# Two rooms for the column sums of a turn

## Chip, cores and metric

The kernel runs on one core of a Trainium2 chip. The metric is the device time of one execution in microseconds (us), the median of several runs.

## What is computed

The reference is a model of four layers on an input of 4 images of 96 channels and 64 x 64 pixels. The change lies in layer 0, a selective scan over the pixels in four directions:

```python
xf = u.reshape(b, DI, L)                              # rows, forwards
xt = u.transpose(0, 1, 3, 2).reshape(b, DI, L)        # columns, forwards
xs = jnp.stack([xf, xt, jnp.flip(xf, -1), jnp.flip(xt, -1)], axis=1)
...
hst = hst * dA + (dt_ * ut)[..., None] * bt[:, :, None, :]
y = jnp.einsum('bkdn,bkn->bkd', hst, ct)
...
y1 = ys[:, 1].reshape(b, DI, w, h).transpose(0, 1, 3, 2)
y3 = jnp.flip(ys[:, 3], -1).reshape(b, DI, w, h).transpose(0, 1, 3, 2)
y = y0 + y1 + y2 + y3
```

Directions 1 and 3 run along columns, so their results have to be transposed before they can be added to those of directions 0 and 2, which run along rows. The sum then goes through a norm and a projection (`scan_outputs`, `output_norm`). Layer 1 is a convolution block, layer 2 a spectral block with a feed-forward part, layer 3 a linear attention with another.

## The kernel before

**Scans.** There are 4 images, 4 directions each, 4 steps of 1024 pixels for each direction, and 24 units in a step (6 groups of 32 channels, with 4 of the 16 states on the 128 partitions each time, 4 such sets): 1536 units. A unit is one product on GpSimd (POOL, L1280), one exponential on ScalarE (ACT, L1287), one scan on VectorE (DVE, L1303) and one product with the output coefficients on DVE or POOL (L1318). TensorE (PE) sums the products over the states (L1341). ACT copies the sums to `yt`, and they are stored to `d_y` in device memory. The operands of the units (`scan_d`, `scan_g`, `scan_B`, `scan_C`) are loaded from device memory on SyncE's queue (SP, L1265), all of them at fixed units of a step.

**The planner.** Function `scans` walks the units one by one; a unit's turn in that walk is called a slot here. After a slot's own instructions it lets other work in. That work is a list of stages in order (`front`, `weights`, `turn`, `conv`, `spectral`, `layer_2`, `product`, `layer_3`, or `layer_3_turn` where a turn shares a stage with layer 3). Only the first stage on the list is served. A stage holds streams (Python generators), a few of them active at once. A stream yields the engine that its next piece needs with a planned time, or `wait(n)`, which holds that stream for n slots. `advance` takes a piece if its engine has room left in this slot. The planner hands out a planned rate of at least 6.0 us a slot; at the start of a step it raises the rate to the work left over the slots left, where that is more. The order of the instructions on every engine is thus fixed when the program is built, by counts and planned times alone. What is left of the stages after the last unit is issued without slots between.

**The turn.** `turn(b)` turns the column sums of image b into rows. There are four of them: for images 0 and 1 in stages of their own, for images 2 and 3 next to layer 3 of the image before. A turn has three thirds of 64 channels. Each one

- loads the sums of directions 1 and 3 for 64 channels and all 4096 pixels into the buffer `t` (L657; two loads of 1 MB, 64 partitions each). `t` is a tile of 128 x 6144 floats from `big`, a pool with two buffers that all stages share;
- waits for 10 slots;
- works on 8 chunks of 512 pixels: `fetch` loads the chunk's rows of direction 0 (L666) and of the skip connection (L667) into the tail of `t`, PE adds both directions while it reads `t` transposed (L672) and adds the rows (L674), ACT copies the result (L678), and it is stored to `d_yt`;
- waits for 2 slots, and the next third is loaded into the same `t`.

For the last image (`early`) the order of the thirds is 2, 0, 1. The chunks of its thirds 0 and 1 wait until direction 0 has come so far (`ready`).

After a turn comes the convolution block of the same image (`conv_block`). Its stream `scan_outputs` waits until enough of the image is scanned (`scanned[b] >= 4 * NCH - c`, which counts chunks over the four directions), then the sum, the norm and the projection follow. `expansions` (L806) and `rows` (L829, L845) are its matmuls; its memory is again two tiles from `big`.

Of the kernel before, what the change touches and what calls it, by code (L numbers as in the profile page):

```python
# [97 lines left out]
def hybrid_kernel(ctx: ExitStack, tc: tile.TileContext, a: dict):  # L98
# [3 lines left out]
    wait = lambda n: ("wait", n, 0, False)  # L102
# [17 lines left out]
    def turns(of):  # L120
        of.append(of.pop(0))
        return of[-1]
# [33 lines left out]
    def const(name, rows=slice(0, 128)):  # L156
        return cst[rows, CS[name]]
# [40 lines left out]
    def big(name):  # L198
        if last_room and turns(thirds) == "last":
            return last_room[0].tile([128, 6144], F32, name=name, tag="big", bufs=1)  # L200
        return bp.tile([128, 6144], F32, name=name, tag="big", bufs=2)
# [6 lines left out]
    def tmp(name, shape=(128, CH), dtype=F32):  # L208

        if last_room and dtype == F32:  # L210
            tag = turns(spare)
            if tag in LAST:
                return last_room[0].tile([128, CH], F32, name=name, tag=tag, bufs=LAST[tag])[:, : shape[1]]
        return bp.tile(list(shape), dtype, name=name, tag="tmp", bufs=TMP)
# [36 lines left out]
    def split(t):  # L251
        return t.rearrange("p (a b) -> p a b", a=RPC)
# [199 lines left out]
    def later(out, t, then=None):  # L452

        to_store.append((out, t, then))
# [8 lines left out]
    def ahead(n, first, items):  # L463

        items, got = list(items), []
        for i, item in enumerate(items):
            while len(got) < min(i + 1 + n, len(items)):
                got.append(first(items[len(got)]))
            yield item, got[i]

    def in_turn(items, make, matmuls, take, evict, depth=2, ready=None):


        made = []

        def oldest():
            p, item, at = made.pop(0)
            yield take[:3] + (at,)
            evict(p, item)
            free()  # L480

        items, n = iter(items), 0
        while True:
            while ready is not None and not ready(n):
                yield wait(1)
            item = next(items, None)
            if item is None:
                break
            yield make[:3] + (n > 0,)
            p = bank()  # L490
            matmuls(p, item)
            made.append((p, item, clock[0]))
            n += 1
            if len(made) == depth:
                yield from oldest()
        while made:
            yield from oldest()
# [148 lines left out]
    def turn(b):  # L646


        im = b % 2
        early = b == B - 1  # L650
        while scanned[b] < (2 if early else 3) * NCH:
            yield wait(1)
        t = big("ya")
        for r in (2, 0, 1) if early else (0, 1, 2):
            lo = 64 * r
            for at, k in ((0, 1), (64, 3)):
                load(t[at : at + 64, :L].rearrange("p (c l) -> p c l", c=NCH),  # L657
                     d_y[k][im][:, lo : lo + 64, :].rearrange("c p l -> p c l"))

            rows = not (early and r == 2)  # L660
            held = slice(0 if rows else 64, 128)

            def fetch(c):
                u = t[:, L + c % 4 * CH : L + c % 4 * CH + CH]
                if rows:
                    load(u[:64], d_y[0][im][c, lo : lo + 64])  # L666
                load(u[64:], d_skip[b][c, lo : lo + 64])  # L667
                return u

            def added(p, of):  # L670
                c, u = of
                mm(split(p[:64]), lhsT=const("two")[:, :64],  # L672
                   rhs=t[:, :L].rearrange("p (w h) -> p h w", h=H)[:, c * RPC : (c + 1) * RPC, :], start=True, stop=False)
                mm(p[:64], lhsT=skips[held, r], rhs=u[held], start=False, stop=True)  # L674

            def stored(p, of):
                s = tmp("yrow")[:64]
                nc.scalar.copy(s, p[:64])  # L678
                later(d_yt[im][of[0]][lo : lo + 64], s)

            chunks = ahead(1, fetch, range(NCH))

            ready = (lambda n: scanned[b] >= 2 * NCH + min(n + 2, NCH)) if early and rows else (lambda n: True)
            yield wait(10)
            yield from in_turn(chunks, pe(2.7, 1), added, ac(0.6), stored, ready=ready)
            yield wait(2)

    def scan_outputs(b, done):

# [401 lines left out]
    def layers_2_and_3(b):  # L1091
# [87 lines left out]
        else:  # L1179
# [3 lines left out]
            Stage("product", 1, product()),  # L1183
            Stage("layer_3", 4 if b == B - 1 else 3, *(layer_3(c) for c in range(NCH))) if b not in (1, 2) else
            Stage("layer_3_turn", 4, turn(b + 1), *(layer_3(c) for c in range(NCH))),
        ]

# [33 lines left out]
    def middle(b):  # L1221

        return ([] if b >= 2 else [Stage("turn", 1, turn(b))]) + conv_block(b)
# [439 lines left out]
```

## Time and profile before

| | |
|---|---|
| median of 3 runs | 6037.62 us (6030.58 to 6042.55) |
| profiled execution | 6029.4 us, its span 6027.6 us |
| mean granted TensorE clock | 0.857 |
| busy: DVE, POOL, PE, ACT | 88%, 86%, 76%, 64% of the span |
| DMA | 1078 MB, 179 GB/s over the span |
| last scan starts | 5545.7 us |
| last convolution ends, last spectral part begins | 5757.4 us |

The page of a profile gives busy times of the engines, the costliest groups of instructions and the transfers. A group's line has the line of the kernel, the engine, the operation, what it writes and reads, and a count; then the total busy time in us, the mean of one in ns, and the idle time of the engine ahead of it with what ended that. A view by stretches gives the same busy times between two moments of the span. DMA issues are listed with the KB of one and the median time from issue to landing.

### The profile page before, as it was taken

What the parts mean: (1) busy time and instruction counts of PE and PEld (TensorE: products, weight loads), DVE (VectorE), ACT (ScalarE), POOL (GpSimd) and SP (SyncE); (2) the same over time, 40 slices, a digit from 0 to 9 for tenths busy, and PEclk for the clock granted to TensorE, in tenths of its full rate; (3) what the DMA queues carried; (4) which work ended last, traced back from release to release, by engine and by line L of the source; (5) the groups of instructions that cost most, each with busy time, mean ns of one, the idle gap of its engine ahead of it and who ended that gap; (6) DMA issues with size and microseconds to landing.
All of it is one profiled execution on the core that took longest, in us unless ns stands there. A gap on an engine that the chain in (4) does not pass through costs nothing. (4 is left out here: it accounts for less than half of the span.)

```text
span 6027.6 us, 78329 instructions
## 1 busy us (share of the span) xinstructions
PE 4564.8 (76%) x27668; PEld 1682.2 (28%) x27668; DVE 5280.0 (88%) x3583; ACT 3856.1 (64%) x6056; POOL 5154.5 (86%) x2219
## 2 busy tenths in 40 slices
PE   6743867755898776686568888768888877779998
PEld 2100212211222642121012246211222642112284
DVE  4999898899999899989999999999999999897045
ACT  4853776764665677877556657777666677665335
POOL 4987898999999999989999999999999999897000
PEclk9855978877999888797689989878999888789999
DMA  5654575667754654466776446557754664674101
GB/s 182 229 177 152 195 227 183 219 211 232 216 161 148 200 194 154 159 196 205 229 238 186 164 159 217 166 175 224 220 173 155 199 199 144 184 239 146 48 16 38
DMA packets 425084, 1078.44 MB, mean 179 GB/s; under 512 B 79378, under 2 KB 81268, under 8 KB 423540
## 3 DMA queue, kind: packets, MB, share of 16 engines
q1 hardware_dynamic: 424692, 1073.44, 56.0%
q8 instruction: 219, 3.59, 0.3%
q14 instruction: 173, 1.42, 0.1%
HBM read 857.02 MB, written 220.66 MB: 179 GB/s over the span
## 5 line engine op out<-in xcount | busy, mean ns | idle before, releaser
L1280 POOL TENSOR_TENSOR scan_w<-scan_g,scan_B 128x1024 f32<-128x1024 f32 x1536 | 3606.5, 2376 | 242.0 <-PE ps_y L1341 112.3
L1287 ACT ACTIVATE ps_da<-scan_d,aneg 128x1024 f32<-128x1024 f32 x1536 | 1714.4, 1116 | 324.3 <-DVE scan_w L1318 176.1
L1318 POOL TENSOR_TENSOR scan_w<-scan_w,scan_C 128x1024 f32<-128x1024 f32 x676 | 1605.4, 2375 | 153.3 <-ACT state L1315 102.4
L1303 DVE TENSOR_TENSOR_SCAN ps_da<-ps_da,state,scan_w 128x1024 f32<-128x1024 f32 x633 | 1483.0, 2343 | 103.8 <-ACT ps_da L1287 92.5
L1341 PE MATMUL ps_y<-scan_w,cst 128*32 128x512 f32 x6144 | 1003.0, 730 | 590.8 <-POOL scan_w L1318 297.8
L1303 DVE TENSOR_TENSOR_SCAN scan_w<-ps_da,state,scan_w 128x1024 f32<-128x1024 f32 x519 | 1214.2, 2341 | 32.9 <-ACT ps_da L1287 30.7
L1318 DVE TENSOR_TENSOR scan_w<-ps_da,scan_C 128x1024 f32<-128x1024 f32 x860 | 1053.1, 1225 | 71.7 <-DMA scan_C<-bc 6.4
L1303 DVE TENSOR_TENSOR_SCAN ps_da<-ps_da,scan_w 128x1024 f32<-128x1024 f32 x227 | 518.4, 2284 | 58.3 <-ACT ps_da L1287 51.1
L1341 PEld LDWEIGHTS ps_y<-scan_w,cst 128*32 128x32 f32 x6144 | 147.2, 117 | 1221.5 <-POOL scan_w L1318 505.1
L1315 ACT COPY state<-ps_da 128x1 f32<-128x1 f32 x654 | 104.1, 159 | 488.4 <-DVE scan_w L1318 486.5
L829 PE MATMUL ps_mm<-h,wd 128*32 128x512 f32 x3144 | 363.5, 593 | 7.0 <-ACT r L169 7.0
L1303 DVE TENSOR_TENSOR_SCAN scan_w<-ps_da,scan_w 128x1024 f32<-128x1024 f32 x157 | 357.8, 2279 | 9.5 <-ACT ps_da L1287 6.9
L567 PE MATMUL ps_mm<-xp,taps 128*128 128x512 f32 x576 | 285.9, 639 | 51.6 <-ACT xp L547 22.2
L806 PE MATMUL ps_mm<-wd,w 128*32 128x512 f32 x1944 | 243.1, 613 | 17.9 <-ACT h L810 8.7
L618 PE MATMUL ps_mm<-xd,dtw 128*128 128x512 f32 x256 | 165.4, 737 | 70.8 <-ACT z L640 43.8
L1315 ACT COPY state<-scan_w 128x1 f32<-128x1 f32 x498 | 93.2, 187 | 192.0 <-DVE scan_w L1303 191.6
L627 ACT ACTIVATE z<-ps_mm 128x512 f32<-128x512 f32 x192 | 114.4, 596 | 148.3 <-PE ps_mm L622 76.5
L633 DVE SCALAR_TENSOR_TENSOR ps_mm<-ps_mm,z 128x512 f32<-128x512 f32 x192 | 131.3, 684 | 87.7 <-ACT z L631 82.6
L888 PE MATMUL ps_mm<-r,cst 128*128 128x512 f32 x220 | 149.4, 768 | 62.4 <-ACT r L885 13.8
L672 PE MATMUL ps_mm<-ya,cst 128*64 128x512 f32 x192 | 183.2, 1043 | 9.1 <-ACT acc L912 8.6
L810 ACT ACTIVATE h<-ps_mm 128x512 f32<-128x512 f32 x258 | 150.6, 596 | 53.8 <-PE ps_mm L806 50.9
L829 PEld LDWEIGHTS ps_mm<-h,wd 128*32 128x32 f32 x3144 | 110.6, 109 | 239.8 <-issue 207.3
(360 smaller groups left out, 6536.9 us busy)
## 6 DMA issues: line engine op xcount, KB each, us to landing
scan_g<-du SPq DMA_DIRECT2D x384, 512.0 KB, 5.0
scan_d<-delta SPq DMA_DIRECT2D x384, 512.0 KB, 5.9
scan_B<-bc SPq DMA_DIRECT2D x256, 512.0 KB, 5.3
scan_C<-bc SPq DMA_DIRECT2D x256, 512.0 KB, 5.2
y<-yt SPq DMA_DIRECT2D x384, 128.0 KB, 2.7
du<-g SPq DMA_DIRECT2D x128, 256.0 KB, 3.0
delta<-z SPq DMA_DIRECT2D x128, 256.0 KB, 2.8
tab<-in_etab SPq DMA_DIRECT2D x112, 256.0 KB, 4.0
```

What stands on the lines that cost most here:

```text
L567: mm(p, lhsT=taps[:, t, 0:128], rhs=window(t, c + e), start=t == 0, stop=t == 8)
L618: mm(p, lhsT=dtw[:, o + 2 * third, 0:128], rhs=xd, start=True, stop=True)
L672: mm(split(p[:64]), lhsT=const("two")[:, :64], rhs=t[:, :L].rearrange("p (w h) -> p h w", h=H)[:, c * RPC : (c + 1) * RPC, :], start=True, ...
L806: mm(p[32 * n : 32 * n + 32], lhsT=w1[:, 32 * g : 32 * g + 32], rhs=xin[:, n : n + 15 : 2, 1 : W + 1], start=True, stop=True)
L810: act(h[:, :, 1 : W + 1], split(p), AF.Relu)
L829: mm(p[32 * n : 32 * n + 32], lhsT=held["wd"][:, groups[i], o, dx, :], rhs=here[i][:, :, dx : dx + W], start=dx == 0, stop=dx == 2)
L1280: nc.gpsimd.tensor_mul(x["w"], x["step"]["g"][x["i"]], x["step"]["B"][x["j"]])
L1287: act(x["da"], x["step"]["d"][x["i"]], AF.Exp, scale=aneg[:, av : av + 1])
L1303: nc.vector.tensor_tensor_scan(x["h"][:, order], x["da"][:, order], x["w"][:, order], start, ALU.mult, ALU.add)
L1315: nc.scalar.copy(step["last"][:, u : u + 1], x["h"][:, end : end + 1])
L1318: x["made"] = engine.tensor_mul(x["w"], x["h"], x["step"]["C"][x["j"]])
L1341: done = mm(y[32 * q : 32 * q + 32], lhsT=const("stack"), rhs=group[m]["w"][:, e * CH : e * CH + CH], start=first, stop=last)
```

## The change

A turn takes two tiles from `big`. The loads of a third (`columns`) go to them in turn. The first third's loads are issued at the start, as before, and 8 slots later, ahead of its chunks, those of the second third. From then on the loads of the next third are issued when a third begins, and 2 slots later its chunks begin. The one wait of 10 slots in each third becomes 8 + 2 in the first third and 2 in the others; the wait of 2 slots behind each third becomes one behind the last.

```diff
         while scanned[b] < (2 if early else 3) * NCH:
             yield wait(1)
-        t = big("ya")
-        for r in (2, 0, 1) if early else (0, 1, 2):
-            lo = 64 * r
+        order = (2, 0, 1) if early else (0, 1, 2)
+        places = [big("ya"), big("yb")]
+
+        def columns(n):
+            t, lo = places[n % 2], 64 * order[n]
             for at, k in ((0, 1), (64, 3)):
                 load(t[at : at + 64, :L].rearrange("p (c l) -> p c l", c=NCH),
                      d_y[k][im][:, lo : lo + 64, :].rearrange("c p l -> p c l"))
 
+        columns(0)
+        for n, r in enumerate(order):
+            t, lo = places[n % 2], 64 * r
             rows = not (early and r == 2)
             held = slice(0 if rows else 64, 128)
 ...
             chunks = ahead(1, fetch, range(NCH))
 
             ready = (lambda n: scanned[b] >= 2 * NCH + min(n + 2, NCH)) if early and rows else (lambda n: True)
-            yield wait(10)
+            if n == 0:
+                yield wait(8)
+            if n + 1 < len(order):
+                columns(n + 1)
+            yield wait(2)
             yield from in_turn(chunks, pe(2.7, 1), added, ac(0.6), stored, ready=ready)
-            yield wait(2)
+        yield wait(2)
```

## Prediction

> **What bounds the kernel now.** I read the page's busy shares first, then its costliest groups, then busy time by stretch for the stages that the change touches, then the transfers beside the column loads, and last the chain that ended last.
>
> ```profile
> PE 4564.8 (76%) x27668; PEld 1682.2 (28%) x27668; DVE 5280.0 (88%) x3583; ACT 3856.1 (64%) x6056; POOL 5154.5 (86%) x2219
> ...
> L1280 POOL TENSOR_TENSOR scan_w<-scan_g,scan_B 128x1024 f32<-128x1024 f32 x1536 | 3606.5, 2376 | 242.0 <-PE ps_y L1341 112.3
> ...
> L1303 DVE TENSOR_TENSOR_SCAN ps_da<-ps_da,state,scan_w 128x1024 f32<-128x1024 f32 x633 | 1483.0, 2343 | 103.8 <-ACT ps_da L1287 92.5
> ```
>
> Each of the 1536 scan units occupies one slot of the program. It costs DVE a scan (2.34 us) and POOL a product (2.38 us), and a second product runs on either: 1.23 us on DVE (L1318, 860 times) or 2.37 us on POOL (676 times). So both engines stay full until the last scan at 5545.7 us. Everything else is filler that the planner slips between slots. After the last scan only TensorE is busy, with what filler is left.
>
> I walked the planner's loop slot by slot, and took the n-th L1303 on DVE as slot n's time. That gives the stretches below. Columns: us of the stretch, then busy time and count of PE, PEld, DVE, ACT, POOL, granted clock, DMA share, GB/s. First turn, third turn with layer 3, fourth turn with layer 3:
>
> ```profile
> 1311.00:1498.60 187.60, 110.55 (x336) 18.75 (x336) 183.33 (x102) 91.77 (x151) 183.53 (x80) 0.73 0.77 229
> 4023.80:4237.00 213.20, 167.97 (x486) 37.81 (x482) 195.50 (x118) 158.54 (x253) 201.17 (x88) 0.87 0.72 215
> 5142.80:5366.50 223.70, 179.46 (x488) 39.30 (x480) 194.08 (x116) 158.22 (x252) 197.53 (x86) 0.81 0.68 201
> ```
>
> The reader is to see that in the turn alone (first line, 60 slots, 3.13 us a slot) DVE and POOL are busy for 98% although the turn itself is mostly waiting: the scans go on. In the third line DVE is busy for 87%: there filler holds up the scans. The end of the program, from the first expansion of the last image's convolution to the last scan, and from there to the end of that convolution:
>
> ```profile
> 5454.00:5545.70 91.70, 87.97 (x548) 26.32 (x540) 87.06 (x53) 56.34 (x77) 83.87 (x36) 1.00 0.43 127
> 5545.70:5757.40 211.70, 200.42 (x1250) 58.48 (x1252) 16.72 (x29) 74.30 (x118) 2.35 (x1) 0.97 0.20 60
> ```
>
> PE is at 96% and 95%: from 5454 us on TensorE sets the time. The transfers around the second column load of the first turn (1360 to 1390 us; KB each, us from issue to landing), and the time of that load alone (1378 to 1384 us):
>
> ```profile
> ya<-y SPq DMA_DIRECT2D x2, 1024.0 KB, 14.3
> scan_C<-bc SPq DMA_DIRECT2D x3, 512.0 KB, 16.7
> ...
> 1378.00:1384.00 6.00, 2.61 (x16) 0.49 (x16) 5.80 (x5) 2.75 (x5) 6.00 (x4) 0.50 1.06 204
> ```
>
> A column load of 2 MB fills all DMA engines at about 200 GB/s, and a scan operand issued near it lands after 16.7 us, not the 5.2 us that the page has as scan_C's median.
>
> **What the Trainium skill says.** "Perfetto Trace Analysis", Identifying the Most-Contended Engine, judges Vector and GpSimd by occupancy, and its Optimization Strategy says that the contended engine may change between regimes. The trace agrees: DVE and POOL at 98% in the turn, PE at 95% at the end. "DMA: Bandwidth & Descriptors", Queues, rings and completion order, says that one issuer's descriptors are consumed in ring order on each DMA engine. The 16.7 us of scan_C behind the column load fits. The same page's Bandwidth table has 1 MB into 128 partitions at 341 GB/s; this load, in two halves of 64 partitions, ran at 204, and that decides.
>
> **The change, part by part.**
>
> *The waits.* Before, each third costs wait(10) and wait(2), 36 slots a turn; after, 8+2, 2, 2 and 2: 16. In the two turns that are stages of their own nothing else may run in those slots, so each stage shrinks from 60 slots to 40. No scan unit vanishes with a slot: 20 slots of 3.13 us are not 63 us saved, only filler moved forward by 20 slots. So what counts is where the earlier filler ends up. The walk gives (slots, before and after):
>
> ```
>                             before       after
> turn of image 0             293-352      293-332
> turn of image 1             757-816      745-784
> turn of image 3 + layer 3   1420-1480    1388-1459
> first expansion, last conv  1508         1504
> planned us left after slots 257          225
> ```
>
> Of the head start of 32 slots at the fourth turn only 4 are left at the first expansion. The last convolution reads scans of its own image: its first outputs wait until 26 chunks are scanned, the next until 28 (slot 1492 in both). After the change 22 of its slots stand empty.
>
> *The end.* It is costed in two ways. The walk takes 88 matmuls out of the part behind the last scan: 48 of L829 (4 pieces of the chain of 2.6 us, 10.4), 40 of L806 (10 pieces of 0.9 to 1.0, 9.5) and two of a norm (about 1): 21 us. But they go under the last 38 slots, where PE is already at 96%, and would stretch those. The second way counts from the first expansion, where TensorE begins to bind: it comes 4 slots earlier, and slots 1504 to 1508 took 13.0 us; the sums of 4 more slots (L1341, 0.65 us of PE a slot) fall behind it, 2.6 us. That is 10.4 us, and up to 3 more, since PE idled 3.7 us in that stretch. I take **-12**, bounds -8 and -21.
>
> *The fourth turn beside layer 3.* Before, the planner is late there and raises its rate to 9.74 us a slot, then 6.26 and 7.07; after, it is 6.0, then 5.09, over 72 slots instead of 61. The cost of haste is read from the stretches as span less the mean of DVE's and POOL's busy time, less the 2.2% that even the idle turn loses: third turn 213.2 - 198.3 - 4.7 = 10.2 us, fourth 223.7 - 195.8 - 4.9 = 23.0. At the lower rate I expect the 10 of the third turn: **-12**, bounds -20 and 0 (if the loss comes from the column loads, it stays).
>
> *Column loads on top of work.* The loads are the same 24 of 1 MB. Eight of the twelve pairs now go out two slots (6.3 us) ahead of a third's first rows (L666, L667), and run beside its stores. On SP's queue they stand ahead of the operands of later slots. The third load waits on SP for the last matmul that reads its room, issued a slot or two before; I put that under 2 us, hidden by operands loaded 4 slots or more ahead. The shortest lead is that of scan_C, four slots and a scan: 4 x 3.13 + 2.34 = 14.9 us, against 16.7 us seen beside a column load, which cost nothing visible. The turn alone gets denser: its DMA share was 0.77 of 187.6 = 144 us of work; 20 slots' operands less (20/24 of 10.5 MB, at the 415 GB/s that they reach, 21 us; stores of y 3) leave 120 in 40 slots of 3.13, 125 us: 96%. In the second turn, at 0.84, it is 133 in 125, at the limit. ACT's copies of rows (L678) wait for PE, PE for the rows, and the next decay (L1287) stands behind those copies. Nothing of before shows this overlap; from the 2 us by which 16.7 already exceeds 14.9 I take about 1 us for each of eight loads, **+8**; bounds 0 and +40 (5 us each, the late rows' 10 us stall half hidden).
>
> *Nothing:* the second room. The two buffers of that size are free when a turn starts (front or spectral part done), and the convolution's load into one waits only for matmuls two slots old. The products split 677 to 676, as before.
>
> **Sum:** -12 - 12 + 8 = -16. The profiled execution took 6029.4 us (span 6027.6 and 1.8 around it), 8.2 below the median of 6037.62: 6029.4 - 16 = 6013.4 there, and 6037.6 - 16 = **6022** as a median.
>
> **Rivals.**
>
> 1. *The transfers stay hidden* (chance 0.25): the overlap costs nothing, and more than 12 at the end is won: -25 to -33, about 6009. For it: PE already stands 7 us at a third's first rows in the first turn, and DVE loses nothing. Against: DMA at 96% and more.
> 2. *Likeliest, as summed* (0.38): -16, between -8 and -24, 6022.
> 3. *The gain is spent* (0.22): no loss goes from the fourth turn, or the overlap costs 15 to 25; -4 to +8, about 6039. For it: the fourth turn's idle time begins right behind column loads, which stay.
> 4. *DMA becomes the bound of the turn* (0.15), slower. One mechanism, in the turns of images 0 and 1: at 96 and 106% the backlog of a column load never drains before the next, scan_C lands after 25 us, and each of eight loads costs 25 - 14.9 = 10 us, less the gap left by the wait, say 5: +40 - 24 = +16, 6054. It decides from 24/8 = 3 us a load, and is measurable from 4.5.
>
> That the change doesn't do what it says is excluded for the waits (the walk shows 40 slots).
>
> **How the numbers follow.** About 0.2% (12 us) is what a measurement of this kernel can tell. Faster than 6025.5: all of rival 1, and some 0.32 of the likeliest case with its 0.38 (it straddles): 0.57. Slower than 6049.7: most of rival 4 and a little of 3: 0.15. The rest, 0.28, within. The range from 6000 to 6050 leaves out the far part of rival 4 and the best of rival 1.
>
> **What would show it.** Right: the two turns take 40 slots and 125 to 133 us each with DVE at 95% or more; the fourth turn with layer 3 has DVE at 92% or more; last scan near 5541 us, last convolution done near 5741 us instead of 5757, and 270 us from there to the end as before. Wrong: DVE below 90% in the two turns with waits for scan_C or ACT (rival 4), or the last scan no earlier (rival 3). If the last scan comes 12 us earlier but the end more than 25, PE was not the limit under the last slots.

## The result and the profile after

The changed kernel takes **6090.05 us** (median; 6086.05 to 6098.0), the kernel before 6036.06 us beside it: a ratio of 1.0088, with an interval of [1.0072, 1.0104]. It is slower by about 54 us, where the forecast was 6022 us and a range up to 6050. Beside the kernel before on another chip it was 6087.66 to 6034.23 us, a ratio of 1.0094 [1.0077, 1.0111].

The page after, busy shares and the two groups of a scan unit (the line numbers are 9 higher than before; the last columns are busy time, mean ns of one, and the engine's idle time ahead of the group with what ended most of it):

```profile
PE 4576.1 (75%) x27668; PEld 1700.4 (28%) x27668; DVE 5279.9 (87%) x3582; ACT 3853.7 (63%) x6056; POOL 5154.8 (85%) x2220
...
L1289 POOL TENSOR_TENSOR scan_w<-scan_g,scan_B 128x1024 f32<-128x1024 f32 x1536 | 3601.6, 2369 | 326.8 <-PE ps_y L1350 179.9
...
L1312 DVE TENSOR_TENSOR_SCAN ps_da<-ps_da,state,scan_w 128x1024 f32<-128x1024 f32 x631 | 1478.7, 2343 | 147.2 <-ACT ps_da L1296 134.7
```

The work is the same, but for one product that moved from DVE to POOL, and as long as before (scan 2343 ns, product 2369 against 2376). What grew is the idle time ahead of it: POOL's before L1289 from 242.0 to 326.8 us, DVE's before this form of the scan from 103.8 to 147.2. DVE is kept waiting by ACT's decay, POOL by PE's sum.

The same six stretches, taken as in the prediction (columns as there: us of the stretch, then busy time and count of PE, PEld, DVE, ACT, POOL, granted clock, DMA share, GB/s). In order: turn of image 0, turn of image 1, third turn with layer 3, fourth turn with layer 3, first expansion to last scan, last scan to the end of the last convolution:

```profile
1314.40:1460.40 146.00, 92.32 (x248) 16.38 (x248) 122.80 (x68) 64.73 (x109) 121.83 (x54) 0.78 0.81 232
2894.50:3033.70 139.20, 92.62 (x248) 16.59 (x248) 123.00 (x69) 61.46 (x85) 120.93 (x53) 0.77 0.83 232
3957.00:4192.20 235.20, 168.55 (x480) 38.71 (x480) 196.88 (x118) 162.17 (x276) 199.97 (x87) 0.84 0.67 194
5114.20:5388.10 273.90, 185.99 (x524) 39.50 (x520) 227.25 (x134) 172.55 (x273) 231.46 (x101) 0.78 0.64 188
5528.20:5634.80 106.60, 102.42 (x647) 33.67 (x649) 100.37 (x63) 69.49 (x99) 97.29 (x42) 0.99 0.46 145
5634.80:5826.90 192.10, 179.91 (x1182) 57.99 (x1174) 14.60 (x24) 66.52 (x105) 2.36 (x1) 1.00 0.20 61
```

The two lone turns have their 40 slots, but take 146 and 139 us for 122 us of work of DVE and POOL. Before, 60 slots took 187.6 us for 183. DVE is busy for 84% and 88% of them, where 95% was expected, and for 83% of the fourth turn, where 92% was expected. The DMA share did not go to 0.96 and over: it is 0.81 and 0.83.

From here on the **loss** of a stage is its length less the mean of DVE's and POOL's busy time, taken record by record with each instruction counted from its recorded start to its end. This is the measure of the prediction without its 2.2%; for the stages above the two agree within 1.6 us.

| us | before | after | after, other chip |
|---|---|---|---|
| loss, turn of image 0 | -0.4 | 21.2 | 16.9 |
| loss, turn of image 1 | -0.2 | 14.9 | 15.2 |
| loss, third turn with layer 3 | 10.5 | 32.6 | 34.7 |
| loss, fourth turn with layer 3 | 24.0 | 40.1 | 39.5 |
| loss, all other stages | 170 | 190 | 180 |
| last scan starts | 5545.7 | 5634.8 | 5623.6 |
| last scan to the end of the span | 481.9 | 461.4 | 462.8 |

On the other chip, whose profiled execution lies near the median, the account is: turns +72, other stages +10, less filler under the scans -5, the end -19; together +59 us between the two spans. So **72 of the 83 us that were newly lost lie in the four turns**, and the expected gain at the end did arrive. Each column is one execution: two of the same kernel differ by 2.5 us in the turns and by 10 in the other stages.

**One loss followed through.** At 1378 us the second third of image 0's turn begins. The DMA issues on SP's queue after, around that moment (start us, us, engine, line, operation):

```profile
1378.99 0.65 SPq L659 DMA_DIRECT2D ya<-y  x1
1379.76 0.67 SPq L1274 DMA_DIRECT2D scan_C<-bc  x1
1380.47 0.61 SPq L1274 DMA_DIRECT2D scan_d<-delta  x1
1381.48 0.50 SPq L459 DMA_DIRECT2D yt<-yrow  x1
1382.18 0.47 SPq L671 DMA_DIRECT2D yb<-y  x1
1385.57 0.45 SPq L672 DMA_DIRECT2D yb<-skip  x1
1386.06 0.60 SPq L671 DMA_DIRECT2D yb<-y  x1
1390.34 0.44 SPq L672 DMA_DIRECT2D yb<-skip  x1
```

The columns of the third third (L659, the second of two loads of 1 MB) and two operands of the scans are issued just ahead of the first rows (L671, L672) of the chunk that PE takes up next:

```profile
1380.09 1.91 PE L677 MATMUL ps_mm<-yb,cst 128*64 128x512 f32 x2
1400.66 1.94 PE L679 MATMUL ps_mm<-yb,skips 128*64 128x512 f32 x2 [18.66 <-DMA yb<-skip]
```

The waits of after between 1386 and 1406 us (who waited for whom: us in total, times, longest):

```profile
PEld ps_mm L679 <- DMA yb<-y: 20.3, 1, 20.3
PE ps_mm L679 <- DMA yb<-skip: 18.7, 1, 18.7
ACT yrow L683 <- PE ps_mm L679: 17.1, 1, 17.1
POOL scan_w L1289 <- PE ps_y L1350: 14.0, 1, 14.0
DVE scan_w L1312 <- ACT ps_da L1296: 13.1, 1, 13.1
```

And ACT's own order after (start, us, engine, line; in brackets the idle time before it and what ended it):

```profile
1384.40 1.11 ACT L1296 ACTIVATE ps_da<-scan_d,aneg 128x1024 f32<-128x1024 f32 x1
1402.63 0.58 ACT L683 COPY yrow<-ps_mm 64x512 f32<-64x512 f32 x1 [17.12 <-PE ps_mm L679]
...
1403.30 1.12 ACT L1296 ACTIVATE ps_da<-scan_d,aneg 128x1024 f32<-128x1024 f32 x1
```

This is the chain to read. The rows of direction 0 land 18.0 us after their issue, those of the skip connection just behind them. PE has started the chunk (L677) and stands before L679, which adds the rows. ACT stands before its copy of that chunk (L683) for 17.1 us. Behind the copy, in ACT's fixed order, is the next decay (L1296), which DVE's scan needs: DVE idles 13.1 us. Behind L679 on PE are the sums (L1350) that free POOL's buffers: POOL idles 14.0 us. The kernel before had a shorter hold of this kind at the first third's rows, in its waits between 1332 and 1348 us:

```profile
PEld ps_mm L674 <- DMA ya<-skip: 9.0, 1, 9.0
```

There DVE did not stop for it, and POOL for 1.6 us. A hold of 9 us was all but covered by what stood ready; one of 18 to 20 us was not. After, one long hold follows in each of the four turns, at slots 315, 767, 1082 and 1410: gaps of 13.1, 6.9, 11.7 and 12.5 us on DVE, and of 14.0, 10.4, 11.8 and 16.6 on POOL. The mean of the two engines makes 48 us, where the turns lost 75 more than before; shorter gaps in the first thirds, at slots 307, 1072, 1393 and 1401, make some 22. On the other chip the holds stand at the same four slots.

"DMA: Bandwidth & Descriptors" of the Trainium skill, Queues, rings and completion order, has each DMA engine take the descriptors of one issuer in ring order. The trace fits. The six transfers issued from 1378.34 to 1382.18 us land in the order of their issue, at 1390.3, 1395.5, 1397.2, 1399.8, 1400.0 and 1400.2 us: ahead of the 128 KB of rows stand 2 MB of columns and 1 MB of operands, at some 200 GB/s. The prediction priced its loads by scan_C and brought late rows in only as its upper bound, at 10 us of which half was to be hidden.

A second limit shows in the same trace. Of the 2510 issues on SP's queue whose eighth predecessor has a recorded landing, none starts before that landing, though 202 of 2510 start before the seventh has landed. So at most eight transfers are under way, and a block that lands late holds back later issues as well: the skip rows of the next chunk go out at 1390.34, when the first column load of 1378.34 has landed after 12.0 us. In this hold it cost little, since the first rows were issued only 0.2 us late by it; the order on the queue decides.

### The profile page after: what moved, and what is told of

Same layout as the page of the kernel before. It is cut to its first block, busy times and chain, and to the rows that moved or that the text cites. A ratio compares the mean times of both kernels' runs of the same rounds, so it can differ in the third digit from the quotient of the medians.

```text
span 6096.2 us, 78316 instructions
## 1 busy us (share of the span) xinstructions
PE 4576.1 (75%) x27668; PEld 1700.4 (28%) x27668; DVE 5279.9 (87%) x3582; ACT 3853.7 (63%) x6056; POOL 5154.8 (85%) x2220
## 5 line engine op out<-in xcount | busy, mean ns | idle before, releaser
L1289 POOL TENSOR_TENSOR scan_w<-scan_g,scan_B 128x1024 f32<-128x1024 f32 x1536 | 3601.6, 2369 | 326.8 <-PE ps_y L1350 179.9
L1296 ACT ACTIVATE ps_da<-scan_d,aneg 128x1024 f32<-128x1024 f32 x1536 | 1715.1, 1117 | 342.9 <-DVE scan_w L1327 188.7
L1327 POOL TENSOR_TENSOR scan_w<-scan_w,scan_C 128x1024 f32<-128x1024 f32 x677 | 1603.8, 2369 | 157.4 <-ACT state L1324 105.5
L1312 DVE TENSOR_TENSOR_SCAN ps_da<-ps_da,state,scan_w 128x1024 f32<-128x1024 f32 x631 | 1478.7, 2343 | 147.2 <-ACT ps_da L1296 134.7
L1350 PE MATMUL ps_y<-scan_w,cst 128*32 128x512 f32 x6144 | 1003.2, 731 | 553.1 <-POOL scan_w L1327 305.7
L1350 PEld LDWEIGHTS ps_y<-scan_w,cst 128*32 128x32 f32 x6144 | 147.3, 117 | 1186.2 <-POOL scan_w L1327 505.9
L1324 ACT COPY state<-ps_da 128x1 f32<-128x1 f32 x653 | 103.8, 159 | 475.0 <-DVE scan_w L1327 473.3
L1312 DVE TENSOR_TENSOR_SCAN scan_w<-ps_da,scan_w 128x1024 f32<-128x1024 f32 x156 | 355.3, 2278 | 18.6 <-ACT ps_da L1296 14.9
L567 PEld LDWEIGHTS ps_mm<-xp,taps 128*128 128x128 f32 x576 | 115.0, 206 | 225.9 <-issue 156.0
```

Of the source, the lines that this page charges most:

```text
L567: mm(p, lhsT=taps[:, t, 0:128], rhs=window(t, c + e), start=t == 0, stop=t == 8)
L1289: nc.gpsimd.tensor_mul(x["w"], x["step"]["g"][x["i"]], x["step"]["B"][x["j"]])
L1296: act(x["da"], x["step"]["d"][x["i"]], AF.Exp, scale=aneg[:, av : av + 1])
L1312: nc.vector.tensor_tensor_scan(x["h"][:, order], x["da"][:, order], x["w"][:, order], start, ALU.mult, ALU.add)
L1324: nc.scalar.copy(step["last"][:, u : u + 1], x["h"][:, end : end + 1])
L1327: x["made"] = engine.tensor_mul(x["w"], x["h"], x["step"]["C"][x["j"]])
```

## Experiments

The theory: rows and other small loads that are needed at once stand behind a block of column loads, PE waits for them, and ACT's and PE's fixed order passes the wait on to the scans. It was set against rivals: the second room itself, the DMA engines' total load, and the place that filler has in the steps of the scans.

**The change again, on another chip.**

> The change itself again, beside the kernel before on this chip: 50 to 60 us slower than before, with the one long hold (15 to 20 us of PE at the second third's first rows) in each turn at the same slots as in its first profile.

Measured: 1.0094 [1.0077, 1.0111], with the losses of the table above. The loss belongs to the program, not to one chip or one execution.

**The next third's columns in pieces behind the rows.** Eight pieces, each behind a chunk's rows, instead of 2 MB ahead of them; the slots stay those of after.

```diff
+        def piece(n, c):
+            t, lo = places[n % 2], 64 * order[n]
+            for at, k in ((0, 1), (64, 3)):
+                load(t[at : at + 64, chunk(c)], d_y[k][im][c, lo : lo + 64])
...
                 load(u[64:], d_skip[b][c, lo : lo + 64])
+                if n + 1 < len(order):
+                    piece(n + 1, c)
                 return u
...
-            if n + 1 < len(order):
-                columns(n + 1)
             yield wait(2)
```

> The change, but the next third's columns come in eight pieces of 2 x 128 KB, one behind each chunk's rows, instead of 2 MB at once ahead of the first rows. The planner's slots are the same as in the change. Theory A (the first rows queue behind the 2 MB; PE, then ACT's copy, then the decays stand, 13 us in one third of each turn and 2 to 6 in others): the stalls go; turn stages back to some 127 us each, 15 to 30 us faster than the kernel before. Theory B (the loss comes from the filler's new place against the operand loads and from a turn that is too dense for the DMA engines): no better than the change, 40 us or more slower than before.

Measured: 6052.45 against 6030.96 us, 1.0035 [1.0023, 1.0048]. The losses of the turns are 8.2, 12.7, 27.8 and 30.8 us: 79.5 in all, against 108.8 after and 33.9 before. The hold of 20 us at the second third becomes 10.6, and the gaps behind it fall from 13.1 to 5.2 us on DVE and from 14.0 to 7.7 on POOL. It missed: theory A had it 15 to 30 us faster than before, and theory B no better than the change; it lies between. The block ahead of the rows carried more than half of the 54 us. What stays: a piece still stands ahead of the next chunk's rows, which are fetched only one chunk ahead.

**The rows earlier.** The rows of a third's first four chunks are fetched ahead of the block, and the others three chunks ahead instead of one. The block stays whole. The thirds of the last image that wait for their scan (`early and rows`) are left as they are: that turn is the control.

```diff
-            chunks = ahead(1, fetch, range(NCH))
+            soon = not (early and rows)
+            chunks, head = ahead(3 if soon else 1, fetch, range(NCH)), []
...
+            if soon:
+                head = [next(chunks)]
             if n + 1 < len(order):
                 columns(n + 1)
             yield wait(2)
-            yield from in_turn(chunks, pe(2.7, 1), added, ac(0.6), stored, ready=ready)
+            yield from in_turn(chain(head, chunks), pe(2.7, 1), added, ac(0.6), stored, ready=ready)
```

> The change, but in each third four chunks of rows are loaded ahead of the 2 MB of the next third (and rows then run three chunks ahead); the last image's thirds 0 and 1 stay as in the change, since their rows are not there yet. Same slots as in the change. Theory A: the 13 us stalls go in the turns of images 0, 1 and 2 and one stays in that of image 3: between 5 and 20 us faster than before. Theory B: no better than the change.

Measured: 6053.54 us, 1.0045 [1.0032, 1.0057]: better than the change, but the 5 to 20 us under the kernel before were missed. The losses of the turns are 5.3, 2.5, 22.6 and 39.2. Its stretches, turn of image 0, of image 1, and the control:

```profile
1311.40:1442.30 130.90, 91.70 (x248) 16.18 (x248) 122.31 (x68) 65.02 (x109) 123.31 (x54) 0.83 0.88 261
2874.20:3002.40 128.20, 90.81 (x248) 16.37 (x248) 122.47 (x69) 61.81 (x85) 123.07 (x54) 0.83 0.89 261
5066.70:5339.80 273.10, 183.79 (x524) 39.42 (x520) 227.26 (x134) 172.78 (x273) 231.69 (x101) 0.80 0.63 189
```

Both lone turns now take what the prediction gave them (125 to 133 us), with the same bytes in fewer us: the DMA share rises to 0.88 and 0.89 while the loss falls. The control is unchanged at 273 us. Its waits between 5150 and 5176 us show the chain of before the edit:

```profile
PEld ps_mm L679 <- DMA yb<-y: 19.2, 1, 19.2
ACT yrow L683 <- PE ps_mm L679: 18.3, 2, 17.5
...
DVE scan_w L1315 <- ACT ps_da L1299: 14.4, 1, 14.4
```

Where the rows go out ahead of the block, between 1366 and 1392 us, the same three engines:

```profile
PEld ps_mm L679 <- DMA yb<-y: 9.4, 1, 9.4
...
ACT yrow L683 <- PE ps_mm L679: 7.3, 4, 2.5
...
DVE ps_da L1315 <- ACT ps_da L1299: 0.8, 1, 0.8
```

PE still waits 9.4 us, but ACT never more than 2.5, POOL 2.5 and DVE 0.8. This is the theory shown by itself: the same loads, the same slots, the same waits in the program; only when the rows go out, against the large loads, differs.

**The two rooms with the long waits.** All 10 slots of wait in each third as before; the second third's columns are then issued at the turn's start, right behind the first's.

```diff
-            if n == 0:
-                yield wait(8)
             if n + 1 < len(order):
                 columns(n + 1)
-            yield wait(2)
+            yield wait(10)
             yield from in_turn(chunks, pe(2.7, 1), added, ac(0.6), stored, ready=ready)
-        yield wait(2)
+            yield wait(2)
```

> Two rooms, the next third loaded when a third begins, but the waits of before (10 and 2 slots in each third), so the slots are those of before. Theory A: the wait of 10 slots covers the load and the rows come after it, so the time is that of before within 10 us, though no load is waited for any more. Theory B: within 10 us as well. A third view, that a second room by itself costs something (a buffer taken from other stages, the load's wait on SP): 15 us or more slower.

Measured: 6055.32 us, 1.0041 [1.0027, 1.0055]; losses of the turns -0.4, 9.0, 22.7 and 28.8. Theories A and B both missed by some 14 us and more; the time fits the third view, that a second room costs something by itself, which the run with pieces below excludes. The waits between 5175 and 5200 us, in the fourth turn, show one of its long holds:

```profile
PEld ps_mm L964 <- DMA xc<-x: 16.4, 1, 16.4
ACT xc L966 <- PE ps_mm L964: 15.7, 1, 15.7
...
DVE ps_da L1310 <- ACT ps_da L1294: 12.9, 1, 12.9
```

It is the same chain with another victim. Two blocks, 4 MB, go out at once, and a small load of layer 3 (`xc`), which shares the stage, stands behind them. The rows need not be the ones that are late.

**One room with the short waits.** The load of a third goes back to its start and to one buffer; the waits are those of after.

```diff
-        places = [big("ya"), big("yb")]
+        places = [big("ya")]
...
-        columns(0)
         for n, r in enumerate(order):
-            t, lo = places[n % 2], 64 * r
+            columns(n)
+            t, lo = places[0], 64 * r
...
-            if n + 1 < len(order):
-                columns(n + 1)
             yield wait(2)
```

> One room as before, but the waits of the change (10 slots in the first third, 2 in the others): the same slots as in the change, with the load in front of its own third. Theory A: each of the second and third thirds stalls for the 2 MB and then the rows, the first does not: as slow as the change or slower, 40 to 100 us above before. If the change's loss came from loading beside work, this would be quicker than the change.

Measured: 6106.51 us, 1.0122 [1.0107, 1.0138]; losses 19.0, 20.6, 39.9 and 44.6. As theory A had it, this is slower than the change. Shorter waits with one room cost about 75 us, and loading ahead gives back about 0.3% (some 17 to 22 us). The wait of 10 slots was not idle time: it was the time in which a block drained with nothing needed behind it.

**The long waits with pieces.** The pieces of the first edit with the waits, and so the slots, of before.

```diff
-            if n == 0:
-                yield wait(8)
-            if n + 1 < len(order):
-                columns(n + 1)
-            yield wait(2)
+            yield wait(10)
             yield from in_turn(chunks, pe(2.7, 1), added, ac(0.6), stored, ready=ready)
-        yield wait(2)
+            yield wait(2)
```

> Two rooms and pieces, one behind each chunk's rows, with the waits of before (10 and 2 in each third): the slots of before. The run with two rooms and the waits kept sent 4 MB at once at the start of a turn and was 24 us slower. Theory A: that was the 4 MB, so here within 8 us of before. If the second room itself costs: again 15 us or more slower.

Measured: 6033.94 against 6037.65 us, 0.9995 [0.9988, 1.0003]; losses -0.4, 3.0, 7.1 and 17.6. Two rooms and the loads spread over the work before cost nothing that can be told. This frees the second room as such. The 24 us of the run with the long waits and whole blocks then lie in the blocks; that it is the 4 MB at the start is argued from where its long holds stand, and was not tested apart.

**All of it together**: rows ahead, three chunks deep, and one piece of the next third behind each chunk that is done; slots of after.

```diff
                 later(d_yt[im][of[0]][lo : lo + 64], s)
+                if n + 1 < len(order) and of[0] + 1 < NCH:
+                    piece(n + 1, of[0] + 1)
...
+            if soon:
+                head = [next(chunks)]
             if n + 1 < len(order):
-                columns(n + 1)
+                piece(n + 1, 0)
             yield wait(2)
```

> The slots of the change; the next third's columns in eight pieces, one behind each finished chunk, and the rows three chunks ahead, the first four of a third two slots before its first matmul (the last image's thirds 0 and 1 keep rows one ahead). Theory A (what costs is any small load that PE needs now and that stands behind large ones on the one queue): the turns alone lose under 3 us each, the third and fourth turn beside layer 3 some 15 and 28; with the tail 20 us shorter that is between 12 faster and 6 slower than before, and 15 to 25 us under the run with pieces alone. Theory B (place of the filler against the operand loads): as the run with pieces, 20 us slower than before.

Measured: 6048.65 us, 1.0024 [1.0015, 1.0033]; losses 5.7, 8.8, 21.5 and 27.5, 63.5 in all. It missed the turns (under 3 us for each lone one was expected) and the time: some 30 us over before stayed in the turns. The first third's columns were still a block at the turn's start. So they were cut too, one piece in each of the eight slots of wait:

```diff
-        columns(0)
...
             if n == 0:
-                yield wait(8)
+                for c in range(NCH):
+                    piece(0, c)
+                    yield wait(1)
```

> As the run before it, with the first third's columns too in eight pieces over the eight slots of its wait. Theory A: layer 3's own loads at the start of the third and fourth turn no longer stand behind 2 MB, 3 to 8 us less than the run before it. Theory B: no difference.

Measured: 6042.82 us, 1.0008 [0.9999, 1.0017], 6 us less, as theory A had it. The fourth turn falls from 27.5 to 17.7 us; it shares its slots with layer 3, whose loads had stood behind that block. In the turns of images 0 and 1 another wait has taken the place, in the waits between 1378 and 1393 us:

```profile
PE ps_mm L681 <- DMA yb<-y: 10.6, 1, 10.6
...
DVE scan_w L1323 <- ACT ps_da L1307: 3.4, 1, 3.4
```

L681 is the matmul that reads the columns: now the last piece of the columns is late, since two slots lie between it and its use. (In this view `yb<-y` names both the columns and the rows, which share the tile.) With four:

```diff
-            yield wait(2)
+            yield wait(4)
             yield from in_turn(chain(head, chunks), pe(2.7, 1), added, ac(0.6), stored, ready=ready)
```

> As the run with all columns in pieces and rows three ahead, but 4 slots instead of 2 ahead of each third's chunks (28 planned us sooner per turn become 14 slots; 225 planned us left at the end, as in the change). In the run before, a third's first matmul still waited some 10 us for the last piece of its columns. Theory A: those holds shrink under the 9 us that cost nothing; the two turns alone lose under 3 us each, the third and fourth under 17; with the tail 18 us shorter, 4 to 15 us faster than the kernel before. Theory B (place against the operand loads decides): within 6 us of the run with 2 slots.

Measured: 6034.64 against 6034.23 us, 1.0005 [0.9995, 1.0015]. Its two lone turns, now 46 slots each:

```profile
1314.10:1462.60 148.50, 97.19 (x280) 17.96 (x280) 144.14 (x80) 74.43 (x124) 145.88 (x64) 0.80 0.82 259
2897.20:3040.60 143.40, 98.66 (x280) 17.79 (x280) 140.32 (x78) 70.08 (x99) 142.01 (x63) 0.80 0.83 259
```

DVE is busy for 97% and 98% again. The losses of the turns are 0.2, -2.0, 14.7 and 18.6 us, 31.5 against 33.9 before, and the end is 17 us shorter than before (465.0 against 481.9). Yet the time is that of before: the losses of the other stages went from 170 to 198 us. So the turns behaved nearly as theory A had it (18.6 where under 17 was expected), but the 4 to 15 us of gain did not come, and the time fits theory B: against the kernel before beside each, it is within 5 us of the run with 2 slots.

**What moving the stages costs.** The kernel before, with four slots of wait behind each turn, so that only the place of the later stages changes:

```diff
             yield from in_turn(chunks, pe(2.7, 1), added, ac(0.6), stored, ready=ready)
             yield wait(2)
+        yield wait(4)
```

> The kernel before with a further wait of 4 slots at the end of each turn, so that all later stages stand against the steps of 24 units as they do in the change (20 slots earlier is 4 later, modulo 24), with the turn itself untouched. The end is worse (331 planned us left instead of 257). If the place of the stages against the operand loads sets their losses: layer 2 of image 0 loses 8 us instead of 2, the second front 18 instead of 30, the first spectral part 3 instead of 14. If the loads of the turn did it: as before.

Measured once: 6092.88 us, most of it at the end, since the filler moves later (53.7 us more behind the last scan). The losses of other stages changed both ways: layer 2 of the first image from 2.2 to 7.1 us, as in the runs with moved stages; the front of the last image from 30.5 to 19.1; the spectral part of the first stayed at 13.5, where 3 was expected. In all they rose by 12 us. So a shift of stages against the 24-unit steps does move single stages by 5 to 11 us, in part as in the changed kernel.

The front of the last image, measured in every run, shows how steady this is. It begins at unit 4 of a step, counted from 0, in both executions of the change, in the five kernels with its slots (slot 652) and here (slot 676), and loses 17.8 to 19.1 us in all eight. At unit 18 (slot 666), before and in both runs with the long waits, it loses 28.7 to 30.5. At unit 6 (slot 654), in the run with 4 slots, it loses 34.8: 16.5 of the 23 us by which that run's other stages lose more than those of the run with 2. So the place alone takes or gives over 10 us in one stage. Why it does, and what loses the rest of the 28 us, was not settled.

The turns are moved by it too: with whole blocks and the old waits, the third turn loses 17.5 us here instead of 10.5, and the fourth 18.2 instead of 24.0.

The runs in one view, in us; the last column is the whole kernel against before:

| kernel | turns' loss | other stages' loss | behind the last scan | ratio |
|---|---|---|---|---|
| before | 33.9 | 170 | 481.9 | 1 |
| after | 108.8 | 190 | 461.4 | 1.0088 |
| after, other chip | 106.3 | 180 | 462.8 | 1.0094 |
| one room, short waits | 124.1 | 187 | 463.5 | 1.0122 |
| pieces behind the rows | 79.5 | 175 | 461.5 | 1.0035 |
| rows earlier | 69.6 | 179 | 464.6 | 1.0045 |
| rows earlier and pieces | 63.5 | 177 | 464.5 | 1.0024 |
| the same, first third in pieces too | 61.0 | 175 | 464.5 | 1.0008 |
| the same, 4 slots ahead of each third | 31.5 | 198 | 465.0 | 1.0005 |
| two rooms, long waits, blocks | 60.1 | 178 | 480.5 | 1.0041 |
| two rooms, long waits, pieces | 27.3 | 174 | 481.3 | 0.9995 |

No version is measurably faster than the kernel before.

## Why the prediction was wrong

**The step that failed is "Column loads on top of work".** It put about 1 us on each of eight loads, +8, with an upper bound of +40. In its place the turns lost 72 to 75 us more than before, some 9 us a load. The landing time was read about rightly: 14.3 us had been read as the median of a block's two loads, and 14.3 is the median of the two at 1378 us. It was set against the wrong deadline. The step took scan_C's lead, 14.9 us, as the shortest. But the rows have a shorter one: in the profile after, PE starts the chunk at 1380.1 us, and its first rows are issued at 1382.2, so their lead is nothing at all. The trace of before held the better price: 16.7 us beside a block, less the 9.0 us that PE stood at a third's first rows at no cost, is 8 us a load, over 60 in all. The text even named the path (ACT's copies wait for PE, PE for the rows, the next decay for the copies), and then priced the transfer by another one. Its upper bound, 10 us of stall with half of it hidden, was passed as well: PE stood 13 to 19 us at the long holds, and DVE 7 to 13 of them.

**"The fourth turn beside layer 3", -12, did not come either.** The loss went from 24.0 to 40.1 us. The slower rate of the planner was there (72 slots), but the haste was not what had cost. With pieces and the slots of before the fourth turn loses 17.6 us at the old rate, and 17.7 in the 72 slots of the change at the lower one. (In the last 96 slots the planner's rate has no lower bound of 6.0 us.) The hedge, that the loss comes from the column loads and stays, is half shown: it did not go, but what made the 24.0 us of before is open, since pieces bring it to 17.6, and the run with moved stages, with whole blocks, to 18.2.

**"The end", -12, was under-sized.** From the last scan to the end of the convolution it went from 211.7 to 192.1 us, and behind the last scan 19 to 21 us were saved. The first way of costing (21 us) had that size, though not its make-up: 28 fewer matmuls of `rows` and 48 fewer of `expansions` stand behind the last scan, where 48 and 40 were counted (and two of a norm, which the 88 leaves out). And the last slots were hardly stretched by what went under them: from slot 1504 to the end of the convolution it was 316.4 us before and is 298.7 after, 17.7 less.

**"The waits"** was right as a step: the slots are those of the walk, and nothing was saved by them. Not in the sum at all was what the other stages lose at their new place in the steps: 10 and 20 us in the two executions of the change, 28 in the version whose turns were repaired. "Nothing: the second room" was right, by the long waits with pieces.

**Rival 4** had the sign and a size near it (10 us a load), with a mechanism that the runs exclude for the changed kernel. The turn was not bound by the DMA engines: its work for them is 0.88 of 130.9 us, 115 us, where 120 and 133 were estimated for the two turns. DVE's waits for scan_C over the whole span are 6.4 us before and 6.3 after. The loss lies in all four turns, not only in the two dense ones; and with the same bytes in fewer us the rows-first run had less of it. Its test, "DVE below 90% with waits for scan_C or ACT", came out true for ACT alone, because the cause ends there too.

## What to carry to other kernels

Before a transfer is moved ahead, list what is issued behind it on the same queue within its landing time, and compare that time with the lead of the most urgent one, not with the lead of the operands that feed the busiest engine. A wait that looks idle may be what keeps a large load apart from small urgent ones; if it is to go, cut the load into pieces and issue the urgent loads first. In a program of fixed order follow a late load along every engine's queue to the one that bounds: what counts is how long a hold the buffers cover. Here, in the turn of image 0, a hold of 9.0 us cost DVE nothing, one of 9.4 cost 0.8, of 10.6 5.2, of 15.2 (at slot 307) 2.7, and of 20.3 13.1: about 9 us were covered, and beyond that it depends on what stands ready.

In such a program a change of one stage also moves all later ones, and that alone took or gave over 10 us in one stage here. A forecast of a few tenths of a per cent has to look at those stages too.

## What the runs showed of the hardware

That a block of 2 MB and the operands behind it hold up a load of 128 KB for 18 us was not expected, nor how far it reaches. While the block drains, the queue moves 211 GB/s at a full DMA share (1382 to 1390 us after), while the whole turn of the rows-first run moved 261 GB/s at a share of 0.88. The delay hits whatever is next in the queue (rows, layer 3's `xc`, or an operand: in the third turn of the rows-first run DVE waits 6.3 us for scan_C), so the same block costs DVE 0 or 13 us by what happens to stand behind it. That no more than eight transfers of the queue are under way at once was not expected either; whether the chip or the way the program signals its transfers sets that number, no run here tells.

Whether the columns would do less harm from another engine's queue was not tried.
